# Layer 1's input convolution with taps accumulated in PSUM, three ScalarE products, standing padded slots and its own list order

## The chip, the core and the metric

The kernel runs on one core of a Trainium2 chip. The metric is the device time of one execution in microseconds (us); the time before is the median of three runs. Engines are TensorE (PE, with its weight loads as PEld), VectorE (DVE), ScalarE (ACT), GpSimd (POOL), and SyncE (SP), which issues the DMA transfers.

## What is computed

Two image layers run one after the other, each as `x = x + layer(group_norm(x))` on an input of 4 images of 128 × 128 pixels with 192 channels. The change lies in layer 1, in the part ahead of its four directional scans:

```python
xz = x @ in_proj_w                       # 192 -> 2 * 192 channels
x_ssm, z = (xz[..., :C], xz[..., C:])
xc = jnp.transpose(x_ssm, (0, 3, 1, 2))
xc = jax.lax.conv_general_dilated(xc, conv_w, (1, 1), 'SAME', feature_group_count=C)
xc = jax.nn.silu(xc + conv_b[None, :, None, None])
x0 = xc.reshape(B, C, L)                               # row by row
x2 = jnp.transpose(xc, (0, 1, 3, 2)).reshape(B, C, L)  # column by column
```

So each channel is projected, then convolved with its own 3 × 3 kernel (nine taps, zeros beyond the edge), then passed through SiLU, and stored twice: in row order and in column order. After the scans an output stage computes `z` from the second half of the projection, gates and projects back.

## The kernel before, in words

`in_conv` (from L990) is this stage. Two images of 192 channels make 384 rows, which fill three blocks of 128 partitions: block 0 holds channels 0 to 127 of the first image, block 2 those of the second, and block 1 channels 128 to 191 of both. There are two such pairs `p`, three blocks `i` and 16 chunks `j` of 8 image rows (1024 pixels): 96 chunks. One chunk does this:

- `load` (L1014 to L1034): SP loads the chunk's input into tiles `x` (4 buffers, 9 rows of 128 pixels). Blocks 0 and 2 need two tiles, one of 128 partitions and one of 64; block 1 needs three, the middle one in two halves of 64 partitions.
- `mm` (L1045, by way of `pair_project`, L974): TensorE projects the x tiles into the PSUM tile `f` (two banks of 512 columns, two buffers). For each half `h` it runs one product over 128 rows and 128 columns, then either one over 64 rows (blocks 0 and 2) or two that fill 64 columns each (block 1). Each 512-column matmul in this type shows as two records.
- `edges` (L1052): GpSimd zeroes the left and right border columns of the padded tile `xi` (3 buffers of 10 × 130), and a border row at an image's top and bottom.
- L1062: ScalarE moves `f` with a bias into `xi`; L1080 keeps the last two rows in a tile `cy`, and L1076 copies them into the next chunk's `xi`. The first chunk of a block projects one more row (L1068, L1071).
- `taps_mm` (L1088): TensorE computes taps 0 and 8 as matmuls with diagonal weights into the PSUM tile `c` (two banks, two buffers).
- L1103 and L1105: VectorE does five taps, `acc = xi * w + ...`. The first reads `c` and writes `acc` in SBUF, the other four read and write `acc`.
- L1109: ScalarE computes taps 2 and 6 as separate products `pr`; GpSimd adds the two (L1113) and adds their sum to `acc` (L1115).
- L1117: ScalarE's SiLU in place on `acc`; L1119: SP stores it in row order; L1121: ScalarE copies it, turned, into the whole-image tile `img` (2 buffers). When a block's 16 chunks are there, SP stores `img` in column order in 16 pieces (L1131).

The order of the work is set by a list scheduler. Every `op(engine, cost, ...)` joins a list with its reads and writes; `Order.emit` then walks it with modelled times and picks for each engine the ready operation of lowest rank (its place in the list less `early`). The result is a fixed instruction order for each engine; at run time each engine follows its own order and waits on semaphores. `Ranked`, which exists already for the scans, takes `early` and a factor on the cost from a table by the name of the operation. A `Slot` is a buffer that the scheduler counts, without allocating a tile.

`pair_project` is used in one other place: the output stage (`outputs`, L1696) calls it for block 1 in each of its 32 chunks.

Of the kernel before, what the change touches and what calls it, by code (L numbers as in the profile page):

```python
# [10 lines left out]
F32 = mybir.dt.float32  # L11
AF = mybir.ActivationFunctionType
ALU = mybir.AluOpType
# [29 lines left out]


DILS = (5, 3)


SCAN_RANKS = {
# [23 lines left out]
def rows(t):  # L72
    return t.rearrange("p (r w) -> p r w", w=W)
# [285 lines left out]
class Maker:  # L359
# [614 lines left out]
    def pair_project(self, outs, i, terms, xs):  # L974


        nc = self.nc
        if i == 1:
            parts = [(1, slice(0, 128), slice(0, 128)), (0, slice(0, 128), slice(0, 64)),
                     (2, slice(0, 128), slice(64, 128))]  # L980
        else:
            parts = [(i, slice(0, 128), slice(0, 128)), (1, slice(32 * i, 32 * i + 64), slice(0, 128))]
        of = {src: lhsT for lhsT, src in terms[i]}
        for h, out in enumerate(outs):
            for q, (src, k, m) in enumerate(parts):
                nc.tensor.matmul(
                    out[m], of[src][k, m], xs(src, h)[k], start=(q == 0), stop=(q > 0 if i == 1 else q == 1)
                )

    def in_conv(self, x1T, gn, xc, win, vec, ident):  # L990

# [1 line left out]


        nc, tc = self.nc, self.tc
        TENSOR, PRODUCTS, VECTOR = (0, 8), (2, 6), (4, 1, 3, 5, 7)
        with ExitStack() as ctx:
            p1 = ctx.enter_context(tc.tile_pool(name="p_1", bufs=1))
            psF = ctx.enter_context(tc.tile_pool(name="p_psF", bufs=2, space=PSUM))
# [3 lines left out]
            for v in range(2):  # L1003
                for n, t in enumerate(TENSOR):
                    nc.vector.tensor_scalar(
                        diag[:, v, n], ident, vec[:, v, V1_CW + t : V1_CW + t + 1], None, ALU.mult
                    )
            od = Order(keep=226, idle=0.250, rate=300e3)
            op = od.op

            def buf(tag, bufs, *shape, pool=p1, stream=None):
# [2 lines left out]
            def load(p, i, j):  # L1014

                lo, hi = (0 if j == 0 else R * j + 1), min(R * j + R, H - 1)
                n0 = lo - R * j
                xs = {}
                for _, src in PAIR_TERMS[i]:
                    t = xs[src] = buf("x", 4, 128, R + 1, W)  # L1020
                    parts = [
                        x for x in self.block_parts(p, src)
                        if src != 1 or i == 1 or x[1] == 2 * p + i // 2
                    ]

# [7 lines left out]
                    op("SP", 0.2, get, writes=[t], size=524e3 if i == 1 or src != 1 else 262e3)  # L1033
                return xs  # L1034

            carry = {}

            def chunk(p, i, j, img):
                terms, bias = pw[p]
                bt, vt = bias[:, i : i + 1], vec[:, i % 2]  # L1040
                xs = load(p, i, j)
                n = R if j < NCH - 1 else R - 1
                t, g = buf("xi", 3, 128, R + 2, W + 2), buf("f", 2, 128, 2, 512, pool=psF, stream="A")
# [8 lines left out]
                def edges():  # L1052
                    nc.gpsimd.memset(t()[:, :, 0:1], 0.0)
                    nc.gpsimd.memset(t()[:, :, W + 1 : W + 2], 0.0)
                    if j == 0:
                        nc.gpsimd.memset(t()[:, 0, :], 0.0)
                    if j == NCH - 1:
                        nc.gpsimd.memset(t()[:, R + 1, :], 0.0)

                op("PE", 3.0, mm, reads=list(xs.values()), writes=[g, t], early=-150)  # L1060
                op("POOL", 0.5, edges, writes=[t])
                op("ACT", 1.1, lambda: nc.scalar.activation(  # L1062
                    t()[:, 2 : 2 + n, 1 : W + 1],
                    g().rearrange("p h (r w) -> p (h r) w", w=W)[:, :n], AF.Identity, bias=bt,
                ), reads=[g], writes=[t])
                if j == 0:
                    g0 = buf("f", 2, 128, 2, 512, pool=psF, stream="B")
                    op("PE", 0.8, lambda: self.pair_project(  # L1068
                        [g0()[:, 0, :W]], i, terms, lambda src, h: xs[src]()[:, 0]
                    ), reads=list(xs.values()), writes=[g0], claims=[t], early=-153)  # L1070
                    op("ACT", 0.3, lambda: nc.scalar.activation(  # L1071
                        t()[:, 1, 1 : W + 1], g0()[:, 0, :W], AF.Identity, bias=bt
                    ), reads=[g0], writes=[t])
                else:
                    c0 = carry["c"]
                    op("ACT", 0.4, lambda: nc.scalar.copy(t()[:, 0:2, 1 : W + 1], c0()),  # L1076
                       reads=[c0], writes=[t], early=327)
                if j < NCH - 1:
                    c = carry["c"] = buf("cy", 2, 128, 2, W)
                    op("ACT", 0.41, lambda: nc.scalar.copy(c(), t()[:, R : R + 2, 1 : W + 1]),  # L1080
                       reads=[t], writes=[c], early=-198)

                def shifted(q, r0=0, r1=R):
                    return t()[:, q // 3 + r0 : q // 3 + r1, q % 3 : q % 3 + W]

                gc, acc = buf("c", 2, 128, 2, 512, pool=psC), buf("acc", 4, 128, T)

                def taps_mm():  # L1088
                    for h in range(2):
                        for q, tap in enumerate(TENSOR):  # L1090
                            nc.tensor.matmul(
                                gc()[:, h], diag[:, i % 2, q], shifted(tap, 4 * h, 4 * h + 4),
                                start=(q == 0), stop=(q == len(TENSOR) - 1),
                            )

                def tap(q, into):
                    nc.vector.scalar_tensor_tensor(  # L1097
                        rows(acc()), shifted(q), vt[:, V1_CW + q : V1_CW + q + 1], rows(into),
                        ALU.mult, ALU.add,
                    )  # L1100

                op("PE", 3.2, taps_mm, reads=[t], writes=[gc])
                op("DVE", 1.5, lambda: tap(VECTOR[0], flat(gc())), reads=[t, gc], writes=[acc])  # L1103
                for q in VECTOR[1:]:
                    op("DVE", 1.3, lambda q=q: tap(q, acc()), reads=[t], writes=[acc])  # L1105
                prs = []
                for q in PRODUCTS:
                    pr = buf("pr", 3, 128, T)
                    op("ACT", 1.12, lambda q=q, pr=pr: nc.scalar.activation(  # L1109
                        rows(pr()), shifted(q), AF.Copy, scale=vt[:, V1_CW + q : V1_CW + q + 1]),  # L1110
                        reads=[t], writes=[pr], early=30)
                    prs.append(pr)
                op("POOL", 2.4, lambda: nc.gpsimd.tensor_tensor(  # L1113
                    prs[0](), prs[0](), prs[1](), ALU.add), reads=[prs[1]], writes=[prs[0]])
                op("POOL", 2.41, lambda: nc.gpsimd.tensor_tensor(  # L1115
                    acc(), acc(), prs[0](), ALU.add), reads=[prs[0]], writes=[acc])
                op("ACT", 1.17, lambda: nc.scalar.activation(  # L1117
                    acc(), acc(), AF.Silu, bias=vt[:, V1_CB : V1_CB + 1]), writes=[acc])
                op("SP", 0.1, lambda: nc.sync.dma_start(  # L1119
                    xc[0][p][i][:, j * T : (j + 1) * T], acc()), reads=[acc], size=524e3)  # L1120
                op("ACT", 2.02, lambda: nc.scalar.copy(  # L1121
                    img()[:, :, R * j : R * j + R], acc().rearrange("p (r w) -> p w r", w=W)
                ), reads=[acc, img], writes=[(img, j)], early=-237)

            for p in range(PAIRS):
                for i in range(3):
# [3 lines left out]
                    for j in range(NCH):  # L1130
                        op("SP", 0.11, lambda p=p, i=i, j=j, img=img: nc.sync.dma_start(  # L1131
                            xc[1][p][i][:, j * T : (j + 1) * T],
                            img()[:, R * j : R * (j + 1)].rearrange("p w h -> p (w h)"),
                        ), reads=[img, *((img, c) for c in range(NCH))], size=524e3, early=-207)

            with tc.manual_schedule(
                engines={
# [817 lines left out]
```

## Time and profile before

| | us |
|---|---|
| Timed runs: median (lowest to highest of 3) | 24250.04 (24228.37 to 24251.32) |
| Profiled execution: device time | 24196.93 |
| Profiled execution: span from first to last instruction | 24195.2 |
| First SiLU of the stage to the last (L1117, 96 of them) | 5839.7 to 6792.4 |
| GpSimd L1113, 96 adds: mean / busy | 3.007 / 288.6 |
| VectorE L1097 on `acc`, 384 taps: mean / busy | 1.868 / 717.4 |
| VectorE L1097 on `c`, 96 taps: mean / busy | 1.277 / 122.6 |

The profile page gives busy time by engine, the span in 40 slices, and the costliest groups of instructions by source line; the trace behind it can be asked for one line, a stretch of time, the waits, the transfers or the instructions in order. In the groups, "out<-in" are the program's tile names, then partitions × elements, then count, busy time, mean of one in ns, and the idle time before them with what ended it. In the timeline, the first two columns are start and duration in us, and a bracket gives the idle time of the engine before the row. All of VectorE's taps stand on L1097, since one helper issues them; they differ by their tiles.

### The profile page before, as it was taken

Reading aid. Unit: us, or ns where it says so; the run is one execution under the profiler, and the core shown is the slowest. Engines: PE = TensorE matmul, PEld = TensorE weight load, DVE = VectorE, ACT = ScalarE, POOL = GpSimd, SP = SyncE. Lnnn points to the kernel's source line nnn. Section 1 sums busy time; section 2 is a strip of 40 time slices with the busy share of each in tenths; the row PEclk is TensorE's granted clock in tenths of the full one; section 3 lists DMA queues with packets and bytes.
Section 4 is the critical chain, followed back from the end, with each engine's and each line's share of the span. In section 5 each row is a group of like instructions: output and inputs, shape, how many; then the busy total and the mean of one; then the engine's idle time right before and its main releaser. Section 6 shows DMA issues by size and latency. Waiting matters only on the chain. (4 is left out here: it accounts for less than half of the span.)

```text
span 24195.2 us, 443358 instructions
## 1 busy us (share of the span) xinstructions
PE 22500.4 (93%) x165124; PEld 8416.1 (35%) x165124; DVE 20661.0 (85%) x13926; ACT 21369.6 (88%) x33575; POOL 20963.4 (87%) x10154
## 2 busy tenths in 40 slices
PE   4999999998889999999999999999999999999988
PEld 2232323222233333333333333333333333333355
DVE  3888888888878988888888888989888888888966
ACT  4999999995679999999999999999999999999944
POOL 3999999893579999999999999999999899999944
PEclk6999999998989999999999999999999999999999
DMA  6998888996666666666666666666666666666654
GB/s 202 249 255 246 249 246 248 246 250 201 213 176 174 178 179 181 171 181 166 169 170 179 177 179 181 178 180 180 176 181 176 167 167 160 170 180 175 172 183 154
DMA packets 2254239, 4633.84 MB, mean 192 GB/s; under 512 B 529152, under 2 KB 778432, under 8 KB 2249024
## 3 DMA queue, kind: packets, MB, share of 16 engines
q1 hardware_dynamic: 2252096, 4605.47, 69.0%
q8 instruction: 1320, 21.63, 0.4%
q14 instruction: 823, 6.74, 0.1%
HBM read 3690.49 MB, written 913.94 MB: 190 GB/s over the span
## 5 line engine op out<-in xcount | busy, mean ns | idle before, releaser
L1438 POOL TENSOR_TENSOR hc<-h,C 128x1024 f32<-128x1024 f32 x6144 | 14287.5, 2369 | 970.4 <-PE Y L1446 590.9
L1432 DVE TENSOR_TENSOR_SCAN h<-dA,st,h 128x1024 f32<-128x1024 f32 x5760 | 13099.7, 2333 | 1369.7 <-ACT dA L1426 834.4
L1394 PE MATMUL f<-D,dT 32*64 32x256 f32 x98304 | 7508.0, 392 | 194.3 <-ACT h L1408 173.4
L1426 ACT ACTIVATE dA<-d,alog 128x1024 f32<-128x1024 f32 x6144 | 7065.8, 1150 | 367.6 <-DVE h L1432 238.9
L1408 ACT COPY h<-f 128x512 f32<-128x512 f32 (+7 forms) x16816 | 6970.9, 505 | 419.0 <-PE f L1394 383.5
L1446 PE MATMUL Y<-hc,sel 128*64 128x512 f32 x24576 | 6592.9, 622 | 415.4 <-POOL hc L1438 319.9
L1394 PEld LDWEIGHTS f<-D,dT 32*64 32x64 f32 x98304 | 3674.6, 132 | 5963.9 <-ACT h L1408 2806.2
L653 POOL TENSOR_TENSOR xs<-xs,pr 128x1024 f32<-128x1024 f32 x1536 | 3639.2, 2372 | 229.9 <-ACT pr L648 163.6
L793 DVE SCALAR_TENSOR_TENSOR hf<-hh,vec,hf 128x512 f32<-128x512 f32 x3072 | 2315.7, 754 | 228.6 <-PE hf L773 137.2
L1446 PEld LDWEIGHTS Y<-hc,sel 128*64 128x64 f32 x24576 | 1273.7, 136 | 3178.0 <-POOL hc L1438 1768.3
L773 PE MATMUL hf<-sa,diag 96*32 96x512 f32 x18432 | 2171.9, 609 | 78.0 <-DVE y L804 40.2
L648 ACT ACTIVATE pr<-xi,vec 128x1024 f32<-128x1024 f32 x1536 | 1703.9, 1142 | 172.6 <-POOL xs L653 169.6
L773 PEld LDWEIGHTS hf<-sa,diag 96*32 96x32 f32 x18432 | 553.4, 110 | 1597.3 <-issue 1337.3
L1432 DVE TENSOR_TENSOR_SCAN h<-dA,h 128x1024 f32<-128x1024 f32 x384 | 852.6, 2274 | 165.7 <-ACT h L1408 79.0
L1267 POOL TENSOR_TENSOR u<-l,u 128x1024 f32<-128x1024 f32 x384 | 908.4, 2366 | 90.0 <-ACT l L1260 89.7
L1257 PE MATMUL f<-pj,w 128*128 128x512 f32 x1536 | 831.0, 654 | 13.2 <-ACT h L1408 10.0
L864 PE MATMUL g<-xz,w 96*128 96x512 f32 x1536 | 762.0, 621 | 26.5 <-DVE y L873 14.0
L1097 DVE SCALAR_TENSOR_TENSOR acc<-xi,vec,acc 128x1024 f32<-128x1024 f32 x384 | 717.4, 1868 | 29.0 <-DVE acc L1097 2.8
L881 PE MATMUL f<-y,wout 128*96 128x512 f32 x1536 | 692.3, 600 | 4.6 <-DVE dA L740 2.7
L1276 PE MATMUL f<-ident,u 128*128 128x128 f32 x3072 | 510.8, 291 | 109.4 <-ACT h L1408 97.7
L1115 POOL TENSOR_TENSOR acc<-acc,pr 128x1024 f32<-128x1024 f32 x96 | 225.7, 2351 | 431.4 <-issue 386.7
L1630 POOL TENSOR_TENSOR s<-s,s 64x1024 f32<-64x1024 f32 x64 | 166.2, 2596 | 403.6 <-ACT s L1645 317.3
(214 smaller groups left out, 20483.6 us busy)
## 6 DMA issues: line engine op xcount, KB each, us to landing
C<-cs SPq DMA_DIRECT2D x4096, 256.0 KB, 5.6
sa<-hpad SPq DMA_DIRECT2D x2304, 276.0 KB, 6.1
D<-image SPq DMA_DIRECT2D x1024, 512.0 KB, 3.9
d<-delta SPq DMA_DIRECT2D x1536, 256.0 KB, 4.2
u<-xc SPq DMA_DIRECT2D x384, 512.0 KB, 4.4
delta<-l SPq DMA_DIRECT2D x384, 512.0 KB, 5.0
hh<-hpad SPq DMA_DIRECT2D x384, 414.0 KB, 6.3
y<-y SPq DMA_DIRECT2D x1152, 128.0 KB, 2.8
```

The source lines that it names most:

```text
L648: op("ACT", 1.1, lambda pr=pr, t=t: nc.scalar.activation(rows(pr()), x()[:, t // 3 : t // 3 + R, t % 3 : t % 3 + W], AF.Copy, scale=v(k, V ...
L653: op("POOL", 2.38, lambda pr=pr: nc.gpsimd.tensor_tensor(o(), o(), pr(), ALU.add), reads=[pr], writes=[o], early=-390)
L773: nc.tensor.matmul(o()[32 * g : 32 * g + 32], diag[:, d, s, k, g], x[:, g, :, c0 : c0 + W], start=(d == 0 and s == 0), stop=(d == 1 and s ...
L793: nc.vector.scalar_tensor_tensor(o3, hh()[:, 1 + dy : 5 + dy, PAD + dx : PAD + dx + W], v(k, V0_K + col), o3, ALU.mult, ALU.add,)
L1257: op("PE", 0.853, lambda g=g, c=c: nc.tensor.matmul(g(), wt()[:, 1, i], x()[:, 512 * c : 512 * c + 512], start=True, stop=True,), reads=[w ...
L1267: op("POOL", 2.312, lambda: nc.gpsimd.tensor_tensor(u(), l(), u(), ALU.mult), reads=[l], writes=[u], rank="du")
L1394: nc.tensor.matmul(gs[n]()[64 * jn : 64 * jn + 64, 256 * a : 256 * a + 256], td()[rt, r // 64, 2 * sb + a], tD()[rt, a].rearrange("t (s n) ...
L1408: nc.scalar.copy(H[:, at : at + nq, 256 * sb : 256 * sb + 256].rearrange("p q (a r s) -> p q a r s", a=2, s=32)[:, :, :, 2 * rp + n], gs[n ...
L1426: op("ACT", 1.056, lambda: nc.scalar.activation(a(), d(), AF.Exp, scale=alog[:, c : c + 1]), reads=[d], writes=[a], table="exp", rank="exp")
L1432: nc.vector.tensor_tensor_scan(hs[:, way], a()[:, way], hs[:, way], 0.0 if at == 0 else s0()[:, q : q + 1], ALU.mult, ALU.add,)
L1438: op("POOL", 2.312, lambda: nc.gpsimd.tensor_tensor(t(), hs, tC(), ALU.mult), reads=[hq, tC], writes=[t], rank="hc")
L1446: nc.tensor.matmul(ym()[64 * th : 64 * th + 64], sel, t()[:, 512 * th : 512 * th + 512], start=(q == 0), stop=(q == NQ - 1),)
```

## The change

Taps: VectorE's five become four (1, 3, 5, 7), each adding into the PSUM tile `c` in place. Tap 4 becomes a third ScalarE product. GpSimd adds the three products (two adds, both among the `pr` tiles, now 5 buffers), VectorE adds their sum to `c`, and SiLU reads `c` and writes `acc` (now 3 buffers).

Padding: the three `xi` buffers become one standing tile `XI` with three slots, whose border columns are zeroed once; per chunk only an image's top or bottom row is zeroed. The last two rows are copied from slot to slot, without `cy`.

Matmul order: `pair_project` runs the 128-row, 128-column product of both halves first, then the narrower ones; `taps_mm` runs tap 0 on both halves, then tap 8.

List order: the scheduler is `Ranked` with a table of its own, other costs, and a model in which transfers have a high rate.

```diff
+CONV_RANKS = {
+    "cin": (-1821, 1.764), "edge": (-1591, 2.948), "img": (-3635, 0.11), "mm": (-2532, 0.617),
...
-        for h, out in enumerate(outs):
-            for q, (src, k, m) in enumerate(parts):
-                nc.tensor.matmul(
-                    out[m], of[src][k, m], xs(src, h)[k], start=(q == 0), stop=(q > 0 if i == 1 else q == 1)
-                )
+        n = len(parts)
+        for q, h in [(0, h) for h in range(len(outs))] + [
+            (q, h) for h in range(len(outs)) for q in range(1, n)
+        ]:
+            (src, k, m), out = parts[q], outs[h]
+            nc.tensor.matmul(out[m], of[src][k, m], xs(src, h)[k], start=(q == 0), stop=(q > 0))
...
-        TENSOR, PRODUCTS, VECTOR = (0, 8), (2, 6), (4, 1, 3, 5, 7)
+        TENSOR, PRODUCTS, VECTOR = (0, 8), (2, 6, 4), (1, 3, 5, 7)
...
-            od = Order(keep=226, idle=0.250, rate=300e3)
+            od = Ranked(CONV_RANKS, 0, 3.29, window=1000, keep=1772, idle=1.347, rate=6.603e+06)
...
+            XIS = 3
+            XI = p1.tile([128, XIS, R + 2, W + 2], F32, name="xi")
+            for n in range(XIS):
+                nc.gpsimd.memset(XI[:, n, :, 0:1], 0.0)
+                nc.gpsimd.memset(XI[:, n, :, W + 1 : W + 2], 0.0)
...
-                    op("ACT", 0.4, lambda: nc.scalar.copy(t()[:, 0:2, 1 : W + 1], c0()),
-                       reads=[c0], writes=[t], early=327)
-                if j < NCH - 1:
-                    c = carry["c"] = buf("cy", 2, 128, 2, W)
-                    op("ACT", 0.41, lambda: nc.scalar.copy(c(), t()[:, R : R + 2, 1 : W + 1]),
-                       reads=[t], writes=[c], early=-198)
+                    op("ACT", 0.3, lambda: nc.scalar.copy(
+                        at[:, 0:2, 1 : W + 1], at0[:, R : R + 2, 1 : W + 1]
+                    ), reads=[t0], writes=[t], rank="cin")
...
-                    for h in range(2):
-                        for q, tap in enumerate(TENSOR):
+                    for q, tap in enumerate(TENSOR):
+                        for h in range(2):
...
-                op("DVE", 1.5, lambda: tap(VECTOR[0], flat(gc())), reads=[t, gc], writes=[acc])
-                for q in VECTOR[1:]:
-                    op("DVE", 1.3, lambda q=q: tap(q, acc()), reads=[t], writes=[acc])
+                for q in VECTOR:
+                    op("DVE", 1.2, lambda q=q: nc.vector.scalar_tensor_tensor(
+                        rows(flat(gc())), shifted(q), vt[:, V1_CW + q : V1_CW + q + 1],
+                        rows(flat(gc())), ALU.mult, ALU.add,
+                    ), reads=[t], writes=[gc], rank="tap")
...
-                op("POOL", 2.4, lambda: nc.gpsimd.tensor_tensor(
-                    prs[0](), prs[0](), prs[1](), ALU.add), reads=[prs[1]], writes=[prs[0]])
-                op("POOL", 2.41, lambda: nc.gpsimd.tensor_tensor(
-                    acc(), acc(), prs[0](), ALU.add), reads=[prs[0]], writes=[acc])
-                op("ACT", 1.17, lambda: nc.scalar.activation(
-                    acc(), acc(), AF.Silu, bias=vt[:, V1_CB : V1_CB + 1]), writes=[acc])
+                for pr in prs[1:]:
+                    op("POOL", 2.31, lambda pr=pr: nc.gpsimd.tensor_tensor(
+                        prs[0](), prs[0](), pr(), ALU.add), reads=[pr], writes=[prs[0]], rank="padd")
+                op("DVE", 1.2, lambda: nc.vector.tensor_tensor(
+                    flat(gc()), prs[0](), flat(gc()), ALU.add), reads=[prs[0]], writes=[gc],
+                    rank="vadd")
+                op("ACT", 1.05, lambda: nc.scalar.activation(
+                    acc(), flat(gc()), AF.Silu, bias=vt[:, V1_CB : V1_CB + 1]),
+                    reads=[gc], writes=[acc], rank="silu")
```

In the built order, SP before issues a block's 16 image stores in a row, with the x loads of the next chunks behind them; after, they stand one a chunk among the next block's loads, except for the last block's 16, which close the stage in both. In block 1 TensorE runs a chunk's projection and then that same chunk's tap matmuls, before and after; in blocks 0 and 2 of the changed order the next chunk's projection stands between the two. In the changed kernel ScalarE's order in blocks 0 and 2 is, for each chunk: SiLU, three products, eviction, image copy, carry copy.

More of the change, by code (lines that the diff above doesn't have):

```diff
@@ L45 @@
 DILS = (5, 3)
+CONV_RANKS = {
+    "cin": (-1821, 1.764), "edge": (-1591, 2.948), "img": (-3635, 0.11), "mm": (-2532, 0.617),
+    "mm0": (2803, 1.433), "padd": (6855, 0.954), "prod": (340, 0.031), "silu": (2639, 0.528),
+    "tap": (-6509, 1.234), "tmm": (-5995, 0.255), "vadd": (-1087, 0.159), "x": (2835, 1.644),
+    "xc0": (726, 1.728), "xc1": (-2403, 45.568), "xi": (-284, 0.007), "xi0": (3933, 0.017),
+}
 SCAN_RANKS = {
@@ L1031, in get @@
                             )
-                    op("SP", 0.2, get, writes=[t], size=524e3 if i == 1 or src != 1 else 262e3)
+                    op("SP", 0.2, get, writes=[t], size=524e3 if i == 1 or src != 1 else 262e3, rank="x")
                 return xs
-            carry = {}
+            carry, turn = {}, {"n": 0}
+            XIS = 3
[3 more added lines that the diff above has]
+                nc.gpsimd.memset(XI[:, n, :, W + 1 : W + 2], 0.0)
             def chunk(p, i, j, img):
@@ L1042, in chunk @@
                 n = R if j < NCH - 1 else R - 1
-                t, g = buf("xi", 3, 128, R + 2, W + 2), buf("f", 2, 128, 2, 512, pool=psF, stream="A")
+                t, g = Slot("xi", XIS), buf("f", 2, 128, 2, 512, pool=psF, stream="A")
+                at = XI[:, turn["n"] % XIS]
+                turn["n"] += 1
                 def mm():
@@ L1050, in mm @@
                     )
[L1052 to L1065, printed above, removed]
+                op("PE", 3.62, mm, reads=list(xs.values()), writes=[g], claims=[t], rank="mm", area=0.75)
                 if j == 0:
@@ L1069, in chunk @@
                         [g0()[:, 0, :W]], i, terms, lambda src, h: xs[src]()[:, 0]
-                    ), reads=list(xs.values()), writes=[g0], claims=[t], early=-153)
+                    ), reads=list(xs.values()), writes=[g0], claims=[t], rank="mm0")
                     op("ACT", 0.3, lambda: nc.scalar.activation(
-                        t()[:, 1, 1 : W + 1], g0()[:, 0, :W], AF.Identity, bias=bt
-                    ), reads=[g0], writes=[t])
-                else:
-                    c0 = carry["c"]
-                    op("ACT", 0.4, lambda: nc.scalar.copy(t()[:, 0:2, 1 : W + 1], c0()),
-                       reads=[c0], writes=[t], early=327)
@@ L1078, in chunk @@
-                if j < NCH - 1:
-                    c = carry["c"] = buf("cy", 2, 128, 2, W)
-                    op("ACT", 0.41, lambda: nc.scalar.copy(c(), t()[:, R : R + 2, 1 : W + 1]),
-                       reads=[t], writes=[c], early=-198)
+                        at[:, 1, 1 : W + 1], g0()[:, 0, :W], AF.Identity, bias=bt
+                    ), reads=[g0], writes=[t], rank="xi0")
+                else:
+                    t0, at0 = carry["t"]
+                    op("ACT", 0.3, lambda: nc.scalar.copy(
+                        at[:, 0:2, 1 : W + 1], at0[:, R : R + 2, 1 : W + 1]
+                    ), reads=[t0], writes=[t], rank="cin")
@@ new lines, in chunk @@
+                if j in (0, NCH - 1):
+                    edge = 0 if j == 0 else R + 1
+                    op("POOL", 0.15, lambda: nc.gpsimd.memset(at[:, edge, 1 : W + 1], 0.0),
+                       writes=[t], rank="edge")
+                op("ACT", 1.0, lambda: nc.scalar.activation(
+                    at[:, 2 : 2 + n, 1 : W + 1],
+                    g().rearrange("p h (r w) -> p (h r) w", w=W)[:, :n], AF.Identity, bias=bt,
+                ), reads=[g], writes=[t], rank="xi")
+                carry["t"] = t, at
@@ L1083, in shifted @@
                 def shifted(q, r0=0, r1=R):
-                    return t()[:, q // 3 + r0 : q // 3 + r1, q % 3 : q % 3 + W]
-                gc, acc = buf("c", 2, 128, 2, 512, pool=psC), buf("acc", 4, 128, T)
+                    return at[:, q // 3 + r0 : q // 3 + r1, q % 3 : q % 3 + W]
+                gc, acc = buf("c", 2, 128, 2, 512, pool=psC), buf("acc", 3, 128, T)
                 def taps_mm():
-                    for h in range(2):
-                        for q, tap in enumerate(TENSOR):
+                    for q, tap in enumerate(TENSOR):
+                        for h in range(2):
@@ L1094, in taps_mm @@
                             )
[L1096 to L1102, printed above, removed]
-                op("DVE", 1.5, lambda: tap(VECTOR[0], flat(gc())), reads=[t, gc], writes=[acc])
-                for q in VECTOR[1:]:
-                    op("DVE", 1.3, lambda q=q: tap(q, acc()), reads=[t], writes=[acc])
+                op("PE", 3.43, taps_mm, reads=[t], writes=[gc], rank="tmm")
@@ L1106, in chunk @@
+                for q in VECTOR:
[3 more added lines that the diff above has]
+                    ), reads=[t], writes=[gc], rank="tap")
                 prs = []
                 for q in PRODUCTS:
-                    pr = buf("pr", 3, 128, T)
-                    op("ACT", 1.12, lambda q=q, pr=pr: nc.scalar.activation(
+                    pr = buf("pr", 5, 128, T)
+                    op("ACT", 1.04, lambda q=q, pr=pr: nc.scalar.activation(
@@ L1110, in chunk @@
                         rows(pr()), shifted(q), AF.Copy, scale=vt[:, V1_CW + q : V1_CW + q + 1]),
-                        reads=[t], writes=[pr], early=30)
+                        reads=[t], writes=[pr], rank="prod")
                     prs.append(pr)
-                op("POOL", 2.4, lambda: nc.gpsimd.tensor_tensor(
-                    prs[0](), prs[0](), prs[1](), ALU.add), reads=[prs[1]], writes=[prs[0]])
-                op("POOL", 2.41, lambda: nc.gpsimd.tensor_tensor(
-                    acc(), acc(), prs[0](), ALU.add), reads=[prs[0]], writes=[acc])
@@ L1119, in chunk @@
+                op("ACT", 1.05, lambda: nc.scalar.activation(
+                    acc(), flat(gc()), AF.Silu, bias=vt[:, V1_CB : V1_CB + 1]),
+                    reads=[gc], writes=[acc], rank="silu")
                 op("SP", 0.1, lambda: nc.sync.dma_start(
-                    xc[0][p][i][:, j * T : (j + 1) * T], acc()), reads=[acc], size=524e3)
-                op("ACT", 2.02, lambda: nc.scalar.copy(
+                    xc[0][p][i][:, j * T : (j + 1) * T], acc()), reads=[acc], size=524e3, rank="xc0")
@@ L1122, in chunk @@
+                op("ACT", 1.9, lambda: nc.scalar.copy(
                     img()[:, :, R * j : R * j + R], acc().rearrange("p (r w) -> p w r", w=W)
-                ), reads=[acc, img], writes=[(img, j)], early=-237)
+                ), reads=[acc, img], writes=[(img, j)], rank="img")
             for p in range(PAIRS):
@@ L1133, in in_conv @@
                             img()[:, R * j : R * (j + 1)].rearrange("p w h -> p (w h)"),
-                        ), reads=[img, *((img, c) for c in range(NCH))], size=524e3, early=-207)
+                        ), reads=[img, *((img, c) for c in range(NCH))], size=524e3, rank="xc1")
             with tc.manual_schedule(
```

## The prediction

> **What bounds the kernel now.** I read the page's groups first: of those on the lines that the diff touches, VectorE's taps (L1097) are the largest. The first and last SiLU of the stage (L1117, 96 of them) start at 5839.7 and 6792.4 us: 95 intervals of 10.03 us. Outside the stage the two kernels have the same instructions in the same order on all five engines, but for one product in the output stage, so the sum is made for these 952.7 us and that product. Next, the line view of the two kinds of tap, and of two older groups that work in PSUM (min/median/max ns; the last line ends in busy time, mean and idle time):
>
> ```profile
> L1097 DVE SCALAR_TENSOR_TENSOR acc<-xi,vec,acc x384: 1283/1285/3392, 5831.9 to 6788.6; 128x1024 f32<-128x1024 f32 x192
> L1097 DVE SCALAR_TENSOR_TENSOR acc<-xi,vec,c x96: 1272/1276/1282, 5830.2 to 6780.2; 128x1024 f32<-128x1024 f32 x96
> ```
> ```profile
> L793 DVE SCALAR_TENSOR_TENSOR hf<-hh,vec,hf x3072: 727/756/758, 582.3 to 5737.7; 128x512 f32<-128x512 f32 x192
> ```
> ```profile
> L738 DVE TENSOR_TENSOR f<-dl,f 128x1024 f32<-128x1024 f32 x192 | 234.8, 1223 | 170.2 <-POOL dl L735 138.3 <-PE f L684 29.8 <-POOL xs L653 0.8
> ```
>
> A tap whose two tensors lie in SBUF takes 1.28 us at best and up to 3.39; the tap that reads c from PSUM never takes over 1.282. The timeline of one steady chunk tells why, and prices ScalarE too:
>
> ```profile
> 5894.61 1.28 DVE L1097 SCALAR_TENSOR_TENSOR acc<-xi,vec,c 128x1024 f32<-128x1024 f32 x1
> 5894.83 2.35 POOL L1115 TENSOR_TENSOR acc<-acc,pr 128x1024 f32<-128x1024 f32 x1 [3.92 <-issue]
> ...
> 5895.92 8.34 DVE L1097 SCALAR_TENSOR_TENSOR acc<-xi,vec,acc 128x1024 f32<-128x1024 f32 x4
> ...
> 5897.21 1.15 ACT L1117 ACTIVATE acc<-acc,vec 128x1024 f32<-128x1024 f32 x1 [2.69 <-POOL acc L1115]
> 5897.22 3.25 POOL L1113 TENSOR_TENSOR pr<-pr 128x1024 f32<-128x1024 f32 x1
> ...
> 5898.27 1.13 ACT L1109 ACTIVATE pr<-xi,vec 128x1024 f32<-128x1024 f32 x1
> ...
> 5899.31 1.09 ACT L1062 ACTIVATE xi<-f,x0b 128x1024 f32<-128x1024 f32 x1
> 5900.30 0.39 ACT L1080 COPY cy<-xi 128x256 f32<-128x256 f32 x1
> 5900.73 0.41 ACT L1076 COPY xi<-cy 128x256 f32<-128x256 f32 x1
> 5901.04 2.01 ACT L1121 COPY img<-acc 128x1024 f32<-128x1024 f32 x1
> ...
> 5902.96 1.15 ACT L1109 ACTIVATE pr<-xi,vec 128x1024 f32<-128x1024 f32 x1
> ...
> 5904.18 1.27 DVE L1097 SCALAR_TENSOR_TENSOR acc<-xi,vec,c 128x1024 f32<-128x1024 f32 x1
> ```
>
> VectorE has no gap from 5894.61 to 5904.18: 9.57 us a chunk, and it is the bound. Four SBUF taps take 8.26 us beside two GpSimd adds, and 5.25 where GpSimd was idle (at 5831.9): 3.0 us of blocking. The PSUM tap runs wholly inside an add and pays nothing. GpSimd's L1113 is stretched too (3.25 against 2.34). The waits view shows what else costs:
>
> ```profile
> ACT acc L1117 <- POOL acc L1115: 253.5, 94, 6.4
> DVE acc L1097 <- PE c L1091: 115.3, 33, 23.3
> PEld c L1091 <- POOL pr L1113: 58.0, 28, 4.3
> PE f L986 <- DMA x<-x1T: 45.6, 10, 14.9
> ```
>
> ScalarE is idle 2.7 us a chunk, behind GpSimd. The 23.3 and 14.9 us are the joints between blocks: 16 image stores in a row (411 to 422 GB/s) hold up the x loads.
>
> **The change, part by part.** A step is the start-to-start time where no gap lies between.
>
> *VectorE.* It keeps four taps, now SBUF + PSUM into PSUM. L793 is that form at 512 columns: 756 ns, steps of 791. Streaming 512 more at the rate between L793 and the 1276 ns PSUM tap (520 ns) gives steps of 1.31; the upper bound is twice L793, 1.58. One add is new, and L738 is its exact form: 1.223, step about 1.26. Sum 4 × 1.31 + 1.26 = 6.5 us (at most 7.6), against 9.57. I take no blocking, since the PSUM tap and L793 (max 758) show none; the bound is the old 3.0.
>
> *GpSimd.* Two adds of 2.35 as before, in SBUF, now products only: 4.7. The two border memsets a chunk (durations 0.12) become six at the start and one row at an image's edge, off the path.
>
> *ScalarE.* Removed: the copy to cy (0.3). Added: a third product. SiLU now reads PSUM; L1062, which also does, costs the same as one from SBUF. By the steps above: SiLU 1.06 + three products 3 × 1.04 + eviction 0.99 + carry copy 0.31 + image copy 1.92 = **7.40**.
>
> *TensorE.* Same matmuls. Four tap matmuls are 8 records of 0.429: 3.43. The product of x takes 4.1: four groups of 0.86 and a change of rows or columns of 0.2 before each. With 128-row products first there are two changes, 3.8. Sum 7.25.
>
> So **ScalarE is late next**, at 7.40, with TensorE 0.15 behind it. Is the loop through the engines longer? SiLU(m-1), one product, the second add, VectorE's add, SiLU(m): 1.06 + 1.14 + 2.35 + 1.22 and hops of 0.1 = 6.2. SiLU(m), tap matmuls into the freed c (two buffers), four taps, add: 1.2 + 3.7 + 5.3 + 1.3 = 11.5 for two chunks. Both fit. In blocks i = 0 and 2 (64 chunks) I take 7.45; bounds are TensorE's 7.25 and 7.9 (VectorE's worst plus a hop and 0.2).
>
> *Blocks i = 1 (32 chunks).* Three x tiles a chunk with four buffers, so two wait for the product before. At 6062.57 SP issued such a group, 0.6 before that product's end. The second half tile, issued 0.5 later, landed 4.70 after its issue; the last tile at 6070.46, 7.9 from the start. In the changed order, as in the old, a chunk's tap matmuls follow its own eviction here, so TensorE runs: product 3.8, eviction with hops 1.4, taps 3.5 = 8.7; by the loads 3.8 + 4.6 + 0.2 = 8.6. Stores add: 1 MiB a chunk, 2.5 us at 415 GB/s, behind the group; were nothing overlapped, 7.9 + 2.5 = 10.4. I take 9.2, nearer the low end since the stores are queued when the group is already on its way; ends 8.7 and 10.4.
>
> By the Trainium skill (SBUF — State Buffer, "The DMA setup-cost knee") a transfer takes about 2 us plus its bytes at 436 GB/s: an estimate of 3.2 us for 512 KB. The rows here say 5.0 to 6.5, in groups; by the page i = 1 would stay at 8.7, 16 us less in the sum.
>
> *Clock.* Before, TensorE paused 1.9 to 2.4 us a chunk, and about one chunk in five met a 3.41 us stretch at half clock (taps 5.33 instead of 3.67 at 5910.80). In i = 0 and 2 the pauses shrink to 0.2 and this goes; in i = 1 about 1.4 us stays; I add 5 us in all (bounds 0 and 32 / 5 × 1.7 = 11).
>
> The Trainium skill (TensorE: Matmul & The Clock Gate, "What's actually happening") ties the half clock to an idle window of about 3.4 us; the row above shows it after 1.9, so by that rule alone the 5 us would be 0.
>
> *List order, SP.* Each chunk's stores still wait for SiLU. The image stores, 16 in a row before, stand one a chunk between the loads of the next block; x is issued ahead of them. The joints (8 to 10 us over a chunk) shrink; I keep 3 us for each of five, bounds 0 and 8. The last 16 stores still end the stage in a row, as before: nothing gained. Start: one tap and one add fewer ahead of the first SiLU, 3 us.
>
> *Output stage.* Its 32 chunks call the same helper for block 1: two changes of 0.2 fewer, 0.4 × 32 = 13 us if TensorE sets that stage's end, 0 if not. It is about 90% busy there (180 of 200 us in the windows view) and waits for GpSimd and VectorE between; I take half, 6.
>
> **Sum.** 64 × 7.45 + 32 × 9.2 + 5 (clock) + 6 × 0.5 (first rows) + 15 (joints) = 794, less one interval: 786. 952.7 − 786 + 3 + 6 = 176 us less. The profiled execution took 24196.93 (span 24195.2), which gives 24021; it lies 53 below the median of the timed runs, 24250, from which I forecast 24075.
>
> **Rivals.**
> 1. *Transfers bound the stage.* i = 1 at 10.4 and, with 1.8 MB a chunk against 1.3 before, 7.9 elsewhere: 506 + 333 + 18 − 7 = 850, with nothing from the outputs 100 less: 24150, or 24130 with i = 1 at 9.8. For: landing times of 6 us in groups. Against: i = 0 loads two chunks ahead.
> 2. *Everything overlaps.* 64 × 7.3 + 32 × 8.7 + 3 + 5 − 7 = 747, and 13 from the outputs: 222 less, 24030.
> 3. *The change does not relieve VectorE.* PSUM taps lose the old 3.0 to GpSimd: 6.5 + 3.0 = 9.5, and only the joints and the clock are won, some 30 us: 24220. Against: 96 taps at most 1.282.
> 4. *Slower.* The block turns round: GpSimd's second add, now between the last product and SiLU, waits out VectorE's row of four taps (5.25). The loop of 6.2 becomes 11.4; 96 × 11.4 − 11 = 1083, 130 more: 24380. It decides from a wait of 3.7 us on, where the loop passes 9.9. For: L1113 at 3.25. Against: it was stretched by SBUF taps; GpSimd's L653 beside L793 stays within 2332 and 2488 ns.
>
> **How the numbers follow.** Forecast 0.58, rival 1 0.20, rival 2 0.12, rival 3 0.05, rival 4 0.05. The likeliest is 24075 (24045 to 24110 by itself); the range 24010 to 24150 takes in rivals 1 and 2. What this kernel's measurement can tell from no change is about 0.2%, 48 us: faster 0.90, same 0.05, slower 0.05.
>
> **What would show it.** Right: taps of 1.28 to 1.32 us with no long ones, GpSimd's adds all near 2.35, ScalarE above 90% busy in i = 0 and 2 with SiLUs 7.4 to 7.5 apart, TensorE waiting for x in i = 1. Wrong: taps above 1.6, adds above 3, SiLU waiting for VectorE's add, or x landings above 8 us in i = 0.

## The result and the profile after

| us | before | after |
|---|---|---|
| Timed runs: median (lowest to highest of 4 each) | 24239.21 (24189.98 to 24251.32) | **23970.01** (23927.62 to 23989.29) |
| Ratio of the timed runs, 95% interval | | 0.9886 [0.9867, 0.9904] |
| Profiled execution: device time / span | 24196.93 / 24195.2 | 23974.17 / 23972.4 |
| First to last SiLU of the stage | 952.7 | 752.3 |
| First load of x in the stage to the first SiLU | 40.1 | 28.1 |
| Last SiLU to the first scan | 84.1 | 82.9 |
| First to last scan instruction | 16135.3 | 16102.3 |
| Output stage, first to last gate product | 1091.1 | 1099.1 |

The change is faster, by 269 us between these medians; the forecast was 175 less, and 23970 lies 40 below the range of 24010 to 24150. The two profiled executions differ by 222.8 us of span: 200.4 in the stage, 33 in the scans, which the change does not touch, 8 given back in the output stage, 2 up to the first SiLU. Those 2 hide a gain: layer 0, also untouched, ran some 14 us longer in the execution after, so that the stage's first load of x was issued at 5813.8 and not at 5799.6; from there to the first SiLU the changed kernel takes 12 us less.

First, the lines of the taps, the adds and SiLU in the changed kernel (durations in ns, min/median/max):

```profile
L1108 DVE SCALAR_TENSOR_TENSOR c<-xi,vec,c x384: 1280/1290/1292, 5835.2 to 6591.5; 128x1024 f32<-128x1024 f32 x192
L1120 POOL TENSOR_TENSOR pr<-pr x192: 2342/2366/2392, 5831.1 to 6590.0; 128x1024 f32<-128x1024 f32 x192
L1125 ACT ACTIVATE acc<-c,vec x96: 1092/1113/1209, 5841.9 to 6594.2; 128x1024 f32<-128x1024 f32 x96
```

No tap and no add is long any more: before, taps reached 3392 and L1113 had a mean of 3007. Next, the timeline of one steady chunk, in block 0 (start, duration; where a row is "x3" or "x4", of all of them):

```profile
5900.53 5.26 DVE L1108 SCALAR_TENSOR_TENSOR c<-xi,vec,c 128x1024 f32<-128x1024 f32 x4 [0.66 <-PE c L1101]
5900.56 1.15 ACT L1125 ACTIVATE acc<-c,vec 128x1024 f32<-128x1024 f32 x1
...
5901.57 3.26 ACT L1115 ACTIVATE pr<-xi,vec 128x1024 f32<-128x1024 f32 x3
...
5902.89 4.69 POOL L1120 TENSOR_TENSOR pr<-pr 128x1024 f32<-128x1024 f32 x2 [2.64 <-ACT pr L1115]
...
5904.69 1.14 ACT L1087 ACTIVATE xi<-f,x0b 128x1024 f32<-128x1024 f32 x1
...
5905.69 2.03 ACT L1130 COPY img<-acc 128x1024 f32<-128x1024 f32 x1
...
5905.90 1.23 DVE L1122 TENSOR_TENSOR c<-pr,c 128x1024 f32<-128x1024 f32 x1
...
5907.57 0.46 ACT L1080 COPY xi<-xi 128x256 f32<-128x256 f32 x1
...
5907.88 1.16 ACT L1125 ACTIVATE acc<-c,vec 128x1024 f32<-128x1024 f32 x1
```

ScalarE has no bracket: it never waits, and from SiLU to SiLU are 7.32 us. VectorE and GpSimd both wait. The windows view says the same for whole stretches in block 0, block 1 and block 2 (stretch, length, then busy time of PE, PEld, DVE, ACT, POOL, then granted clock, DMA share, GB/s):

```profile
5860.00:5950.00 90.00, 88.50 (x206) 35.26 (x205) 79.10 (x63) 89.97 (x86) 58.64 (x28) 1.00 0.63 196
5975.00:6090.00 115.00, 98.32 (x260) 37.22 (x260) 82.98 (x65) 99.42 (x92) 61.25 (x29) 0.99 0.92 289
6110.00:6220.00 110.00, 110.00 (x247) 43.93 (x246) 96.42 (x77) 109.94 (x107) 70.60 (x33) 1.00 0.79 254
```

In blocks 0 and 2 ScalarE is busy all the time and TensorE nearly so; in block 1 neither is, and a chunk takes 8.53 us (median). There TensorE's own timeline shows the reason:

```profile
6019.16 3.70 PE L1101 MATMUL c<-xi,diag 128*128 128x512 f32 x8 [1.20 <-ACT xi L1087]
6022.70 3.75 PE L997 MATMUL f<-x,x0w 128*128 128x512 f32 x12
6027.69 3.70 PE L1101 MATMUL c<-xi,diag 128*128 128x512 f32 x8 [1.24 <-ACT xi L1087]
```

Taps, projection, a wait of 1.24 for the eviction of that projection, taps again: 8.53 from row to row, and no wait for x. The waits view of the stage (total, times, longest) agrees:

```profile
PE c L1101 <- ACT xi L1087: 34.4, 26, 2.5
...
PEld f L997 <- DMA x<-x1T: 2.7, 5, 0.9
```

x costs 2.7 us in the whole stage, where it cost TensorE 45.6 before; and nobody waits long for VectorE (SiLU: 2.9 us in 3 waits).

### The profile page after: what moved, and what is told of

It is laid out like the page before. It is cut to its first block, busy times and chain, and to the rows that moved or that the text cites. A ratio compares the mean times of both kernels' runs of the same rounds, so it can differ in the third digit from the quotient of the medians.

```text
span 23972.4 us, 443228 instructions
## 1 busy us (share of the span) xinstructions
PE 22369.9 (93%) x165124; PEld 8429.1 (35%) x165124; DVE 20440.2 (85%) x13926; ACT 21413.4 (89%) x33581; POOL 20892.9 (87%) x9968
## 5 line engine op out<-in xcount | busy, mean ns | idle before, releaser
L1120 POOL TENSOR_TENSOR pr<-pr 128x1024 f32<-128x1024 f32 x192 | 451.3, 2366 | 346.4 <-ACT pr L1115 335.8
L1108 DVE SCALAR_TENSOR_TENSOR c<-xi,vec,c 128x1024 f32<-128x1024 f32 x384 | 495.3, 1290 | 131.7 <-PE c L1101 103.1
```

## The experiments

The measure that tells the theories apart is the stage, first to last SiLU of the profiled execution. It leaves out the run-up from the first load of x to the first SiLU, which is named where it matters. For the whole time a ratio to the kernel before is given with its 95% interval.

**The two kernels again.** No edit.

> The kernel before, once more, to learn how far two sets of runs of one kernel lie apart, and how far its stages move from execution to execution. Theory A (the whole gain comes from the convolution stage, and the rest of the difference of the medians is scatter of the untouched scan stage): ratio 1.000 within 0.2%; the convolution stage again 950 to 956 us from first to last SiLU, the scan stage anywhere within 16090 to 16150 us. Theory B (the change also shortens the untouched scan stage by some 30 us): the scan stage comes out at 16125 to 16145 again.

> The changed kernel, once more. Theory A: 200 us less in the convolution stage and nothing elsewhere, so a ratio of 0.9917 (0.990 to 0.993); first to last SiLU 750 to 755 us; the scan stage within 16090 to 16150. Theory B: ratio 0.9885 as first measured, and a scan stage near 16100 in this profile too.

> The changed kernel a third time. Theory A (the gain is the convolution stage's 200 us; what first measurements show beyond it is scatter of the untouched scan stage with TensorE's clock): first to last SiLU 750 to 755 us, the scan stage anywhere in 16100 to 16310, and a ratio nearer 0.992 than 0.9886. Theory B (the change makes the scan stage quicker too): scan stage near 16120, ratio 0.9885.

| | ratio [95%] | median (lowest to highest) | stage | scans |
|---|---|---|---|---|
| before again | 1.0004 [0.9988, 1.0019] | 24232.54 (24178 to 24331, 12 runs) | 962.4 | 16218.6 |
| after again | 0.9910 [0.9894, 0.9927] | 24013.53 (24001 to 24028, 6 runs) | 752.3 | 16141.7 |
| after, third time | 0.9926 [0.9897, 0.9955] | 24030.82 (23984 to 24146, 6 runs) | 756.1 | 16224.7 |

The changed kernel's stage comes back within 4 us, the old one's within 10 (952.7 and 962.4). Two expectations were missed: "before again" with 962.4 for its stage (950 to 956) and 16218.6 for its scans (16090 to 16150); the third run of the changed kernel lies 1 us above its 750 to 755. From the first load of x to the last SiLU the kernel before takes 992.8 and 1001.8, the changed one 780.4, 780.6 and 784.1: 209 to 221 us less. The whole time does not come back as well: both later medians lie inside the predicted range, 44 and 61 us above the first. Over all runs the changed kernel has a median of 24009 (16 runs, 23928 to 24146), the kernel before 24240 (85 runs, 24164 to 24391). The difference of 231 is the 209 to 221 of the stage with its run-up, and 10 to 22 that the profiles do not assign to any part for good.

Where the scatter sits is seen in the scans, here in two executions with the same scan instructions; first the changed kernel, then the kernel of "Two products" below (windows view, first to last scan):

```profile
6677.00:22779.00 16102.00, 15297.64 (x130352) 5736.86 (x130346) 14276.57 (x6718) 15242.23 (x26925) 15152.15 (x6523) 0.99 0.66 175
```
```profile
6685.00:22991.00 16306.00, 15520.54 (x130352) 5777.62 (x130348) 14285.05 (x6718) 15246.73 (x26925) 15153.13 (x6523) 0.97 0.65 173
```

Same counts, VectorE, ScalarE and GpSimd busy within 9 us, but TensorE busy 223 us longer at a lower granted clock, and the scans 204 longer. Over 14 profiles the scans run from 16102 to 16306. In 81 runs of the kernel before that list their clock, the time follows the mean granted clock with a correlation of -0.98, about 19 us per 0.001.

**The lock.** Theory: the taps' accumulator in PSUM takes VectorE out of GpSimd's way. Rivals 3 and 4: it does not matter, or the loop turns round. The edit puts the accumulator back in SBUF and leaves all else of the change:

```diff
-                        rows(flat(gc())), shifted(q), vt[:, V1_CW + q : V1_CW + q + 1],
-                        rows(flat(gc())), ALU.mult, ALU.add,
+                        rows(acc()), shifted(q), vt[:, V1_CW + q : V1_CW + q + 1],
+                        rows(acc()) if a else rows(flat(gc())), ALU.mult, ALU.add,
...
-                    flat(gc()), prs[0](), flat(gc()), ALU.add), reads=[prs[0]], writes=[gc],
+                    acc(), prs[0](), acc(), ALU.add), reads=[prs[0]], writes=[gc],
...
-                    acc(), flat(gc()), AF.Silu, bias=vt[:, V1_CB : V1_CB + 1]),
+                    acc(), acc(), AF.Silu, bias=vt[:, V1_CB : V1_CB + 1]),
```

> The changed kernel with one thing put back: VectorE's four taps and its add run in the SBUF tile acc again (the first tap reads the PSUM tile c, the others and the add have both tensors in SBUF), in the changed list order with three products. Theory A (the PSUM operand is what frees VectorE from GpSimd): taps with two SBUF tensors up to 3.4 us, GpSimd's adds stretched too, 9.3 to 9.6 us a chunk, first to last SiLU 890 to 920 us, ratio about 0.995. Rival (fewer taps and the new list give the gain, not PSUM): taps stay near 1.29, 7.3 us a chunk in blocks 0 and 2, ratio as of the changed kernel.

Stage 993.0, 10.44 us a chunk, ratio 1.0010 [0.9992, 1.0028]: all of the gain is gone, and the chunk is dearer than the 9.3 to 9.6 expected. The lines of its taps and adds, then its timeline:

```profile
L1108 DVE SCALAR_TENSOR_TENSOR acc<-xi,vec,acc x288: 1283/3260/3284, 5820.4 to 6817.6; 128x1024 f32<-128x1024 f32 x144
...
L1108 DVE SCALAR_TENSOR_TENSOR acc<-xi,vec,c x96: 1266/1275/1282, 5819.1 to 6811.7; 128x1024 f32<-128x1024 f32 x96
```
```profile
5900.18 1.27 DVE L1108 SCALAR_TENSOR_TENSOR acc<-xi,vec,c 128x1024 f32<-128x1024 f32 x1
...
5901.49 7.89 DVE L1108 SCALAR_TENSOR_TENSOR acc<-xi,vec,acc 128x1024 f32<-128x1024 f32 x3
...
5902.63 5.67 POOL L1120 TENSOR_TENSOR pr<-pr 128x1024 f32<-128x1024 f32 x2 [4.78 <-ACT pr L1115]
...
5909.48 1.23 DVE L1122 TENSOR_TENSOR acc<-pr,acc 128x1024 f32<-128x1024 f32 x1
...
5910.63 1.27 DVE L1108 SCALAR_TENSOR_TENSOR acc<-xi,vec,c 128x1024 f32<-128x1024 f32 x1
5910.74 1.15 ACT L1125 ACTIVATE acc<-acc,vec 128x1024 f32<-128x1024 f32 x1 [2.99 <-DVE acc L1122]
```

VectorE has no bracket: its own row of four taps and an add fills the 10.45 us from one tap on `c` to the next. The three SBUF taps, beside two adds of 5.67, take 7.99 from their start to VectorE's add, where 3 × 1.32 = 4.0 would do: 4.0 us of blocking, against 3.0 in the kernel before. ScalarE's wait of 2.99 is a wait for that row. So this is the blocking that rival 3 feared, paid by taps in SBUF. The loop of rival 4 is not seen here either: GpSimd's adds are over at 5908.30, 1.2 us before VectorE's add, which waits for nothing. The tap that reads `c` never passes 1.282, in the same kernel and beside the same adds. The Trainium skill (SBUF — State Buffer, "Who interferes with whom") says that a VectorE instruction with two SBUF inputs contends with a GpSimd instruction that reads SBUF, and one with at most one such input, outside its two-port modes, does not; the 3260 and the 1290 ns agree.

**What bounds the chunk now.** Two edits that each make another engine the longest. First, tap 4 goes back to VectorE:

```diff
-        TENSOR, PRODUCTS, VECTOR = (0, 8), (2, 6, 4), (1, 3, 5, 7)
+        TENSOR, PRODUCTS, VECTOR = (0, 8), (2, 6), (4, 1, 3, 5, 7)
```

> The changed kernel with tap 4 given back to VectorE: five taps in PSUM and an add there (5 x 1.31 + 1.26 = 7.8 us), two products on ScalarE (6.3 us), one add on GpSimd. Theory A (the stage's pace is the sum of its busiest engine): blocks 0 and 2 go from 7.33 (ScalarE) to 7.8 (VectorE), block 1 stays at 8.5, first to last SiLU 780 to 790 us. Rival (the pace is set by the loop through GpSimd's two adds): faster than 7.33, since one add is gone.

Two products: 7.82 us a chunk in blocks 0 and 2, stage 769.6 (780 to 790 was expected), ratio 0.9915 [0.9891, 0.9940]. The prediction's steps for VectorE give 5 × 1.31 + 1.26 = 7.81. In 90 us of block 0 (DVE is the third busy time):

```profile
5860.00:5950.00 90.00, 83.63 (x196) 32.41 (x194) 87.20 (x70) 74.23 (x69) 28.55 (x14) 1.00 0.59 184
```

The taps, all in PSUM, take at most 1291 ns. So the third product is worth 17 us of the 200, and with two products, as before, the change from SBUF to PSUM already removes the lock. The stage came out shorter than expected because block 1 did not stay at 8.5: its two medians are 8.0 and 8.3 (means 8.6 and 8.8). Second, the matmul order goes back:

```diff
-        for q, h in [(0, h) for h in range(len(outs))] + [
-            (q, h) for h in range(len(outs)) for q in range(1, n)
-        ]:
+        for h, out in enumerate(outs):
+            for q, (src, k, m) in enumerate(parts):
...
-                    for q, tap in enumerate(TENSOR):
-                        for h in range(2):
+                    for h in range(2):
+                        for q, tap in enumerate(TENSOR):
```

> The changed kernel with the old order of the matmuls (each half complete before the next, in the projection and in the tap matmuls). Theory A: TensorE, at 7.25 us a chunk, stands just under ScalarE's 7.33; two more changes of 0.2 make it 7.65, so blocks 0 and 2 go to 7.6 to 7.7 and block 1 to 8.9, first to last SiLU 780 us. Rival (TensorE has slack, the order is worth nothing here either): 752 as before.

Blocks 0 and 2 at 7.65 us with TensorE busy 89.68 of 90 us (the sum of the old rows is 4.1 + 3.5 = 7.6), block 1 at 9.86 and 10.0 (8.9 was expected), stage 808.3 (780 was expected), ratio 0.9932 [0.9910, 0.9954]. Block 1 has a new wait, in TensorE's timeline:

```profile
6025.70 2.02 PE L994 MATMUL f<-x,x0w 128*128 128x512 f32 x4
6028.53 3.14 PE L994 MATMUL f<-x,x0w 128*64 128x512 f32 x8 [0.81 <-DMA x<-x1T]
```

After two records of the first half the narrow products need the last x tile, and it has not landed. TensorE is idle for 0.81 us, but the late product starts 1.88 after its partner of 64 columns (6026.65), beside which it runs in the changed kernel (6024.51 and 6024.52). With the 128-row products of both halves first the last tile is needed 0.86 us later in the row, and the next loads go out sooner: the first 1.9 us after the projection's start (6024.61, for 6022.70), right behind the 128-row products, against 5.0 here (6030.69, for 6025.70). Both help to hide the tile; no run separates them. The run-up before the first SiLU is 37.2 with the old order, against 28.1. The projection's order alone, in the kernel before:

> The kernel before, with only the new order of the matmuls in the projection helper (128-row products of both halves first). Theory A: TensorE is not the bound of the old convolution stage, VectorE is, so the stage stays at 950 us; in the output stage 0 to 13 us; ratio 0.9995 (0.998 to 1.0). Rival: TensorE's saved 0.3 to 0.4 us a chunk count in both stages, some 30 + 13 us: ratio 0.998.

Stage 949.6, ratio 1.0002 [0.9982, 1.0022]: against 952.7 and 962.4 not clear of scatter. The order that is worth next to nothing while VectorE is the bound is worth 56 us where TensorE is close to it. (The 56 include the tap matmuls' old order; their row is 3.70 with either.)

**The list.** The changed sums with the old scheduler settings, and the old sums with the new ones:

```diff
-            od = Ranked(CONV_RANKS, 0, 3.29, window=1000, keep=1772, idle=1.347, rate=6.603e+06)
+            od = Order(keep=226, idle=0.250, rate=300e3)
```

> The changed arithmetic (taps in PSUM, three products, standing slots, new matmul order) with the old scheduler parameters, so the old kind of list order, image stores in a row included. Theory A (the engines' sums give most of the gain, the list a smaller part): 7.3 to 7.8 us a chunk inside blocks 0 and 2, 8.5 to 9 in block 1, but joints of 8 to 10 us over a chunk: first to last SiLU 800 to 830 us against 752. Rival (the list order is most of the gain): 880 us or more.

> The kernel before with only the new list order (the table of ranks and the parameters that go with it), taps in SBUF, two products, old matmul order. Theory A: VectorE beside GpSimd stays the bound at 9.57 us a chunk; only the joints between blocks shrink, 952 becomes 915 to 935 us from first to last SiLU. Rival (the list gives most of the gain): 850 us or less.

New sums, old list: 846.3 (800 to 830 was expected), ratio 0.9944 [0.9929, 0.9959]. Old sums, new list: 924.8, ratio 1.0012 [0.9991, 1.0032]. The list takes 28 us off the old sums (952.7 to 924.8) and 94 off the new ones (846.3 to 752.3). Of the 28 some are lost ahead of the first SiLU, which comes 52 us after the first load of x and not 40; from that load on the old sums gain 16 us (25 against the second execution), and the ratio shows none of it. The steady chunk of blocks 0 and 2 is nearly the same with either list (9.58, and 7.47 against 7.33). With the old list and the new sums the joints are 11.5 to 13.1 us, and in each block behind a joint one chunk takes 18 to 31 us, the third or the fourth: these five long chunks are most of the 94. The waits say that the loads behind 16 stores in a row are still what TensorE waits for there:

```profile
PE f L997 <- DMA x<-x1T: 72.4, 5, 18.1
```

**Buffers and copies.** A fifth buffer for x, paid for with the fifth `pr`:

```diff
-                    t = xs[src] = buf("x", 4, 128, R + 1, W)
+                    t = xs[src] = buf("x", 5, 128, R + 1, W)
...
-                    pr = buf("pr", 5, 128, T)
+                    pr = buf("pr", 4, 128, T)
```

> The changed kernel with five x buffers instead of four (and four product buffers instead of five, for the room). Theory A (block 1 is bound by TensorE's own row: product, wait for the eviction, taps): block 1 stays at 8.5 us a chunk. Rival (block 1 is bound by the x loads): it falls to 8.0 or less. In both, blocks 0 and 2 stay at 7.3 to 7.4 unless the fourth product buffer is missed.

Stage 820.9, ratio 0.9929 [0.9912, 0.9946]. Block 1 stays at a median of 8.53, with the same wait of 1.24 for the eviction and none for x in its steady chunks, so it is not short of x buffers. Blocks 0 and 2 go to 8.33, since ScalarE, the bound, now waits about a microsecond in each chunk for VectorE's add, and that for GpSimd (waits in 90 us of block 0, 11 chunks):

```profile
DVE c L1122 <- POOL pr L1120: 21.3, 11, 1.9
...
ACT acc L1125 <- DVE c L1122: 10.5, 11, 1.3
```

The standing slots undone: own `xi` tiles, borders zeroed in every chunk, the copies to `cy` and back, and `acc` with 2 buffers instead of 3:

```diff
-                        at[:, 0:2, 1 : W + 1], at0[:, R : R + 2, 1 : W + 1]
-                    ), reads=[t0], writes=[t], rank="cin")
+                    op("ACT", 0.3, lambda: nc.scalar.copy(t()[:, 0:2, 1 : W + 1], c0()),
+                       reads=[c0], writes=[t], rank="cin")
...
+                    op("ACT", 0.3, lambda: nc.scalar.copy(c(), t()[:, R : R + 2, 1 : W + 1]),
```

> The changed kernel with the old padding: xi tiles of their own with borders zeroed for each chunk, and the last rows copied to cy and from there (two acc buffers instead of three, for the room). Theory A (ScalarE is the bound at 7.33): one copy of 0.3 us more, 7.63 in blocks 0 and 2, block 1 unchanged at 8.5, first to last SiLU 770 to 780. Rival (ScalarE is not the bound): 752 to 757.

Stage 789.2 (770 to 780 was expected), 7.78 a chunk, ratio 0.9929 [0.9906, 0.9953]. The copy costs 0.45 and not the 0.3 of its own step: ScalarE's timeline has

```profile
5904.91 1.11 ACT L1083 ACTIVATE xi<-f,x0b 128x1024 f32<-128x1024 f32 x1
5906.06 0.41 ACT L1089 COPY cy<-xi 128x256 f32<-128x256 f32 x1
5906.37 2.00 ACT L1129 COPY img<-acc 128x1024 f32<-128x1024 f32 x1
```

The copy reads what the eviction just wrote and starts 1.15 after it; in the changed kernel the next instruction there, the image copy, starts 1.00 after. So 0.15 goes to the dependent step and 0.31 to the copy. The kernel before had such a pair in the rows of the prediction: from 5900.30, the copy to `cy`, to 5900.73, the copy that reads it, are 0.43.

**A version meant to be faster.** In block 1 ScalarE has slack that TensorE's row leaves it, so two products there should let the scheduler put the next projection ahead of the taps:

```diff
+                PRODUCTS, VECTOR = ((2, 6), (4, 1, 3, 5, 7)) if i == 1 else ((2, 6, 4), (1, 3, 5, 7))
```

> The changed kernel with two products and five VectorE taps in block 1 alone, where the list then puts the next chunk's projection ahead of a chunk's tap matmuls, so that TensorE has no wait for its own eviction. Theory A (there, loads are next behind TensorE's own row, since the DMA engines are 92% busy): block 1 at 8.0 to 8.6, blocks 0 and 2 at 7.33, first to last SiLU 735 to 752. Rival (only TensorE's own row counts): block 1 at 7.8, VectorE's sum, 725.

Stage 774.9 (735 to 752 was expected), ratio 0.9931 [0.9909, 0.9953]. The projection does stand ahead in places, but its x tiles then come late. TensorE in one such place:

```profile
6063.46 3.86 PE L997 MATMUL f<-x,x0w 128*128 128x512 f32 x12 [2.84 <-DMA x<-x1T]
```

ScalarE's eviction at 6060.70 had waited 6.18 us for the projection ahead of that. Block 1 has a median of 8.57 and means of 9.4 and 9.6. None of these versions is faster than the changed kernel.

## Why the prediction was wrong

The mechanism was the forecast's; the time missed the range. From the predicted 24021 for the profiled execution to the 23974 measured are 47 us, and from there to the medians another 58.

- **VectorE, GpSimd: right.** Taps in steps of 1.32, the add at 1.23, GpSimd's adds at 2.37, no long ones.
- **ScalarE late next: right.** 7.33 against a sum of 7.40 and 7.45 taken: 64 × 0.12 = 8 us. "TensorE 0.15 behind" holds too: TensorE is busy 88.5 of 90 us. (The parts named for the old product of x give 4.24 and not 4.1; with the old order back, its chunk took 7.65.)
- **Block 1: mis-sized, the largest term.** "I take 9.2" for its chunks, and 8.53 came: 32 × 0.67 = 21 us. The row 3.8 + 1.4 + 3.5 = 8.7 was right and stands alone. The half microsecond added for stores ahead of the loads was wrong, and the sign "TensorE waiting for x in i = 1" did not show, though the queue did get slower: 512 KB of x took a median of 6.9 us from issue to landing in that stretch, and the DMA engines were 92% busy. With the 128-row products first the next loads go out sooner and the narrow products, which need the last tiles, come later; that part of the change was counted only as two tile changes less. When it was undone, the wait that the prediction feared was there (0.81 us in the chunk shown).
- **The Trainium skill's estimate for transfers** (SBUF — State Buffer, "The DMA setup-cost knee"). By its 3.2 us, block 1 would have stayed at 8.7, which is close to what came, but not for that reason: the landings of 6.9 do not agree with it.
- **Clock, joints, first rows: 23 us taken, some 17 came** (752.3 less the chunks, 64 × 7.33 + 32 × 8.53 − 7.33 = 734.8). In the steady stretches the granted clock was 0.99 to 1.00, and the joints are 7.3 to 11.5 us. Five stretches of 3.41 us at half clock are left in the stage, each after a pause of TensorE of 2.3 to 2.7 us: at most 1.7 us each, 8.5 in all, and how much of that the stage waits for is not shown. By the idle window of about 3.4 us that the Trainium skill names (TensorE: Matmul & The Clock Gate, "What's actually happening") there would be none; these rows do not agree with it.
- **Start: 3 us taken, 12 came**, between the first load of x and the first SiLU. With the old matmul order the run-up is 37.2 of the old 40.1, so most of the gain goes with that order, which the prediction did not count there.
- **Output stage: 6 us taken, nothing to be seen.** It took 1091 and 1105 before, 1099, 1114 and 1101 after; between the two profiles of the result it is 8 longer.
- **The failed step: "How the numbers follow".** The stage's terms were 34 us too high and the start's 9, the output stage's 14 too low: 29 in all, well inside the range. But the range was made of cases of the stage alone. It had no term for the scatter of what the change does not touch, which gave 19 us between the two profiles (the scans 33 less, layer 0 14 more). And the "53 below" of the profiled execution was added to the forecast as if it were a fixed distance, when it was one draw: the after-profile lies 4 above its median. These 19 and 58 are 77 of the 105 us between 24075 and 23970.

With the two later medians, 24014 and 24031, the forecast misses by 61 and 44, inside the range. So it is in part bad luck that the first median fell outside, but not that all three lie below the forecast: over all runs the change is worth 231 us and not 175, and 43 of these 56 are the terms of the stage and the start. The median of all 16 runs, 24009, is just at the range's end.

Rival 1 (transfers) had its condition, a full queue, and not its price. Rival 2 gave 747 for the stage and 24030 in all: nearest of all in the stage, with its 13 from the outputs missing. Rival 3 is excluded by the 1290 ns; the blocking it feared came only where the taps lie in SBUF. The loop of rival 4 was seen in no run.

## What to carry to other kernels

Where VectorE and GpSimd slow each other down, ask whether VectorE's running sum can live in PSUM: here that alone took a tap from up to 3.4 to 1.29 us, and the rest of the change was worth most of its time only after it (matmul order within the scatter before and 56 us after, list 28 and 94). When summing a row of an engine, take the wait that the trace shows and do not add one for a resource that is merely busy; ask which instruction needs the late tile, and what runs before it. And a range needs the scatter of the part that is not changed: with 23 ms of unchanged work, a saving of 209 to 221 us in the stage and its run-up was measured as 217, 222 and 269.

## What the runs showed of the hardware

- The same scan instructions in the same order took 16102 to 16306 us, with TensorE's mean granted clock in that stretch between 0.989 and 0.973. Why the clock differs between executions stays open; no run here tells it.
- With the DMA engines 92% busy at 289 GB/s, 512 KB of x took a median of 6.9 us from issue to landing (block 1, after); with 73% it took 5.9 (block 1, before) and with 63% 3.6 (block 0, after). At 92% TensorE did not wait for x in the rows shown.
- Stretches of 3.41 us at half clock followed pauses of TensorE of 1.9 us (5908.92 to 5910.80, before) and of 2.3 to 2.7 us (five in the stage after).
- ScalarE: an instruction that reads what the one ahead wrote starts 0.15 us later than one that does not (1.15 against 1.00, behind an eviction of 128 × 1024).
